# A state-space convolution with a 4-bit feed-forward on one core: reloads on another queue, a lag between chains, filler matmuls, earlier tables and staggered last chains

## The chip, the core and the metric

One core of one Trainium2 chip. The metric is device time of one execution in microseconds (us); lower is better. The engines are called by what they do in this kernel: TensorE (PE in the profile) runs matmuls, VectorE (DVE), ScalarE (ACT) and GpSimd (POOL) do elementwise work, SyncE (SP) issues transfers. ScalarE and GpSimd can issue transfers too.

## The reference, cut to what matters

```python
# x: [32, 64, 1024]; H = 64 heads, L = 1024, N = 64 states; lengths per batch row
K = 2 * real(einsum('hn,hnl->hl', Cs, exp(dtA * arange(L))))     # kernel of each head
y = causal_convolution(x * mask, K) + x * mask * D               # by FFT in the reference
y = y * mask
gate = y @ Wg;  up = y @ Wu                                      # 1024 x 2752, 4-bit, groups of 128
inter = gate * sigmoid(gate) * up
out = x + float16(inter @ Wd)                                    # 2752 x 1024, 4-bit, groups of 128
```

The rows of the products are the 2048 pairs (head, batch row), and their columns run along the 1024 positions.

## The kernel before, in words

Work is held with positions on partitions and the 2048 pairs along the free axis, cut into four blocks of 512 (16 heads each). A convolution is a product with Toeplitz tiles: the head's kernel is computed in factors (`tables` and `factors` on VectorE and ScalarE, `make_kernel` on TensorE), written to a padded DRAM tensor `kpad`, and read back as a Toeplitz tile `t0` of 512 KB per head (`toeplitz`, by SP). `conv_head` does 24 matmuls of a head; after every second head the pair is masked and split into a high and a low float16 part (`xh`, `xl`).

The weights are unpacked to 8 bits, and scales are applied in PSUM: a chain accumulates one group of 128 rows (four matmuls of 128x512), then VectorE or ScalarE multiplies the PSUM tile by the ratio of two scales, and the next group is added. `gu_one` and `gu_pair` are chains of gate and up, `dn_pair(k, blk, place)` is a chain of the down product: 256 of the 1024 output rows (k from 0 to 3) for block `blk`, 22 groups. Its inputs are `ihl` (21 groups, high and low parts, one block at a time) and `ic` (the last group). The chains of gate and up make the products of two blocks at once. Those of the first go into `ihl`, those of the second into the DRAM tensor `spill`. When the fourth chain of block 0 (or 2) has passed group g, `dn_pair` issues a reload of `ihl[:, g]` from `spill` (256 KB) for block 1 (or 3), and the chains of that block wait, in the order in which the program is written, until the reload of their group has been issued.

`roll` writes that order out: it takes chains from a list, holds three in PSUM (four in the stages called wide, when convolutions do not need the banks), and lets each do one group in turn. Between the groups it lets side work go on at given rates. Stage 0 and 1 are gate and up chains of one block; 2 the pairs for blocks 0 and 1; 3 and 4 the down chains of blocks 0 and 1, with the convolutions of blocks 2 and 3 (heads 32 to 63) at their side; 5 the pairs for blocks 2 and 3; 6 and 7 the down chains of blocks 2 and 3. A planner (`dve`, `act`, `pe`, with fixed costs) decides only which engine gets each rescale.

Ahead of `roll` lies the lead: the parameters, the kernels of heads 0 to 15, the convolution of block 0 with other work hung in at given steps (`events`), and matmuls without a use that keep TensorE occupied (`busy`). Heads 16 to 31 run at the side of stage 0; the tables and the kernel of heads 24 to 31 are `group_24`. At the end of a down chain the scaled result `o` is added to the residual `xr` and stored.

The lines of the profile: 524 is the Toeplitz load, 547 the matmul of a head, 617 and 619 the rescale of a pair chain, 636 and 639 that of the other chains, 679 and 680 the matmuls of `gu_pair`, 723 and 724 those of `dn_pair`, 731 the reload, 742 to 744 the output, 750 the residual load, 424 and 426 the matmuls of `make_kernel`, 866 the filler. Tile `chq` is a chain's PSUM tile, `cq` that of two heads, `kq` that of a kernel.

Of the kernel before, what the change touches and what calls it, by code (L numbers as in the profile page):

```python
# [10 lines left out]
F16 = mybir.dt.float16  # L11
F8 = mybir.dt.float8e4
# [5 lines left out]
ALU = mybir.AluOpType  # L18
# [6 lines left out]
GH, GI = 8, 22  # L25
# [6 lines left out]
MAGIC = 12582912.0  # L32
RATES = {"first": (0.5, 4.6), "fill": (1.0, 0.8), "convs": 1.9}
HOP, MM, LANDING = 220.0, 215.7, 6000.0
DVE_ROOM, ACT_ROOM = 1200.0, 1500.0
LOG2E = 1.4426950408889634
LN2_HI = 0.693359375
# [126 lines left out]
def decay_tables(nc, pool, co, cst, h0):  # L164
    xd = pool.tile([128, 8, 64], F32, name=f"xd{h0 // 8}", bufs=1, tag=f"xd{h0 // 8 % 4}")
    for h in range(8):
        nc.scalar.activation(xd[:, h, :], cst[:, 0:64], AF.Exp, scale=co["na"][:, h0 + h:h0 + h + 1])
    return xd
# [89 lines left out]
class Core:  # L258
# [451 lines left out]
    def dn_pair(self, k, blk, place):  # L710
        nc = self.nc
        q = self.psum("chq", place)
        ready = self.bank(place)
        for g in range(GI):
            while blk % 2 == 1 and g < 21 and not self.loaded.get((blk, g)):
                yield
            if g in (0, 8, 16):
                self.need(("dn", k, g // 8))
            self.pe((4 if g < 21 else 2) * MM, ready)
            for j in range(2):  # L720
                lw = self.wd[k][:, g, 128 * j:128 * j + 128]
                if g < 21:
                    nc.tensor.matmul(q[:, j], lw, self.ihl[:, g, 0], start=(g == 0), stop=False, skip_group_check=True)  # L723
                    nc.tensor.matmul(q[:, j], lw, self.ihl[:, g, 1], start=False, stop=False, skip_group_check=True)  # L724
                else:
                    nc.tensor.matmul(q[:, j], lw, self.ic[blk % 2], start=False, stop=True, skip_group_check=True)
            if g < 21:
                ready = self.rescale_two(q, self.rdn[:, 2 * k:2 * k + 2, g:g + 1])
                self.passed[blk, g] = self.passed.get((blk, g), 0) + 1
                if blk % 2 == 0 and self.passed[blk, g] == 4:  # L730
                    nc.gpsimd.dma_start(self.ihl[:, g], self.spill[g])
                    self.loaded[blk + 1, g] = True
                yield
        xr = self.res[k] if blk == 3 else self.residual(self.fw, 2 * k, blk)
        o = self.fw.tile([128, 2, 512], F16, name="o", bufs=2)
        self.bank_free[place].append(self.act(1180, self.tp + HOP) + HOP)
        for j in range(2):
            n = 2 * k + j
            if blk == 3 and j == 1 and k > 0:
                nc.vector.tensor_scalar(o[:, j], q[:, j], self.ldn[:, n:n + 1], None, ALU.mult)  # L740
            else:
                nc.scalar.activation(o[:, j], q[:, j], AF.Copy, scale=self.ldn[:, n:n + 1])
            (nc.gpsimd if blk < 3 or (j == 0 and k < 3) else nc.vector).tensor_tensor(xr[:, j], xr[:, j], o[:, j], ALU.add)
            (nc.gpsimd if blk < 3 else nc.sync).dma_start(self.io["out"][128 * n:128 * n + 128, 512 * blk:512 * blk + 512], xr[:, j])
        yield

    def residual(self, pool, n0, blk):
# [7 lines left out]
def roll(c, items, sides, wide):  # L755
    items, active = list(items), []
    used = {"a": 0, "b": 0}
    stage, credit = 0, {}

    def place(s):  # L760
        if used["b"] < PLACES["b", "pair"]:
            return "b"
        if s in wide and used["a"] == 0:
            return "a"
        return None

    def begin():
        nonlocal stage
        where = place(items[0][0]) if items else None
        if where is None:  # L770
            return None
        s, make = items.pop(0)
        if s != stage:
            c.forced = True
            for side, _, must in sides.get(stage, ()):
                for _ in side if must else ():
                    pass
            stage, c.forced = s, False
        if where == "a":
            c.banks("a", "pair")  # L780
        used[where] += 1
        active.append([s, make(where), where, 0])
        return active[-1]

    recent = []

    def round_of():
        if items:
            return list(active)
        resting = recent[-2:] if len(active) > 2 else recent[-1:]  # L790
        return [min((a for a in active if a not in resting or len(active) == 1), key=lambda a: a[3])]

    while items or active:
        begin()
        for a in round_of():
            recent.append(a)
            a[3] += 1
            try:
                next(a[1])
            except StopIteration:  # L800
                active.remove(a)
                used[a[2]] -= 1
                new = begin()
                if new:
                    new[3] += 1
                    next(new[1])
            now = min([o[0] for o in active] + [stage])
            if now not in wide and used["a"] == 0:
                c.banks("a", "single")
            for side, rate, paced in sides.get(now, ()):  # L810
                credit[side] = min(credit.get(side, 0.0) + rate, 2.0 if paced is None else 99.0)
                while credit[side] >= 1 and (paced is not None or c.room()):
                    credit[side] -= 1
                    next(side, None)
# [3 lines left out]
def tile_ssm_ffn(ctx, tc, io):  # L818
    nc = tc.nc
    c = Core(ctx, tc, io)  # L820
# [13 lines left out]
    kg_stack = ExitStack()  # L834
    kg = kg_stack.enter_context(tc.tile_pool(name="kg", bufs=1))
# [22 lines left out]
    xd = [decay_tables(nc, kg, co, c.cst, h0) for h0 in (0, 8)]  # L858
# [4 lines left out]
    def busy(h0, n):  # L863
        e1, e2 = (e.rearrange("p h n -> p (h n)") for e in c.fac[h0])
        for _ in range(n):
            nc.tensor.matmul(c.psum("wq", "b")[:, 0, :128], e1, e2, start=True, stop=True)
# [11 lines left out]
    c.masks()  # L878
    tc.no_sync_barrier()

    def ratios_gu():
        c.rgu, c.lgu = c.scale_ratios(c.sgu, NT, GH, "gu", [
            (0, 21, 0, 128, 1.0), (21, 42, 0, 128, 0.0625), (42, 43, 0, 64, 1.0), (42, 43, 64, 128, 0.0625)])
# [17 lines left out]
    def load_16():  # L901
        c.us[4] = c.conv_load(16)

    events = {7: kernel_8, 56: ratios_gu, 87: load_16, 75: lambda: c.make_kernel(kg, 16, 8, "b")}
    for i, _ in enumerate(c.conv(0)):
        if i in events:
            with c.after("dve" if i == 56 else None):
                events[i]()
        if i % 8 == 0 and 32 <= i <= 104:
            next(unpack_it)  # L910

    def second():
        with c.after("dve"):
            ratios_dn()
        for h in range(16, 22):
            c.t0[h] = c.toeplitz(h)
        for h in range(16, 32):
            forced, c.forced = c.forced, True
            while h >= 22 and 24 not in c.known:
                next(group_it)  # L920
            c.forced = forced
            yield from c.conv_head(h)

    def group_24():
        yield from c.tables(kg, 24, 8)
        yield from c.factors(kg, 24, 8, xd[3])
        for _ in range(2):
            yield
        c.make_kernel(kg, 24, 8, "a")
        yield  # L930
        kg_stack.close()
        wdp = ctx.enter_context(tc.tile_pool(name="wdp", bufs=1))
        c.wd = [wdp.tile([128, GI, 256], F8, name=f"wd{k}") for k in range(4)]
        yield

    group_it = group_24()

    def third():
        tiles = [c.cv.tile([128, 2, L], F16, name="t0", bufs=3) for _ in range(3)]
# [66 lines left out]
    def residuals():  # L1006
        take = c.scratch(c.x[0])
        c.res = [c.residual(take, n0, 3) for n0 in (0, 2, 4, 6)]
        yield

    convs_it = convs()
# [10 lines left out]
    def one(s, b):  # L1022
        return [(s, lambda where, i=i: c.gu_one(i, b, where)) for i in range(4)]

    def pairs(s, i0):
        order = [ct for i in range(i0, 21) for ct in (i, 21 + i)] + [42]
        chains = [(s, lambda where, ct=ct: c.gu_pair(ct, where)) for ct in order]
        if s == 2:
            for at, h0 in ((34, 40), (30, 32)):
                chains.insert(at, (s, kernel_item(h0)))  # L1030
        return chains
# [4 lines left out]
    items = one(0, 0) + one(1, 1) + pairs(2, 4) + down(3, 0) + down(4, 1) + pairs(5, 0) + down(6, 2) + down(7, 3)  # L1036
# [63 lines left out]
```

## Time and profile before

| | |
|---|---|
| Time of the runs | 1098.02 us median of 3 (1097.51 to 1101.98) |
| Profiled execution | 1101.47 us, its span 1099.7 us, mean granted clock 0.985 |
| TensorE busy | 1030.9 us, 94% |
| VectorE, ScalarE, GpSimd busy | 817.5, 760.1, 275.9 us |
| Chain that ended last | PE 72%, DVE 10%, DMA 6%, ACT 6%, issue 5% |
| Reloads | 42 of 256 KB on GpSimd's queue, median 3.0 us from issue to landing |
| Toeplitz loads to `t` | 48 of 512 KB on SP's queue, median 4.1 us |

A window row gives, for a stretch of the span, the busy time of each engine and how many instructions it ran, then the clock granted to TensorE (1.00 is full), the share of time in which the transfer engines were busy, and GB/s. A timeline row gives start, duration, engine, line, operation, tiles, and in brackets how long the engine had been idle before and what ended that. The rows of waits give who waited for whom, the total, how many times, and the longest. The end of a matmul is modelled; back to back, matmuls of 128x512 start every 0.216 us, though each is shown as 0.38.

### The profile page before, as it was taken

The page shows a single profiled execution, that of the slowest core. Times are in us where ns is not written, and L with a number is a line of the kernel's source. Part 1 is how long each engine was busy: PE and PEld are TensorE (multiplying, and loading weights), DVE is VectorE, ACT ScalarE, POOL GpSimd, SP SyncE. Part 2 cuts the span into 40 slices and gives each one's busy share as a digit, 9 for nine tenths or more (in the row PEclk, how much of TensorE's full clock was granted, in tenths as well). Part 3 has the DMA queues.
Part 4 walks back from the last instruction along what each step waited for, and adds up shares of the span by engine and source line. Part 5 has one row for each costly group of instructions (what it writes and reads, how often), then busy time and mean ns, then how long its engine had stood idle before and what let it go on. Part 6 is the DMA issues. An engine that isn't in the chain of part 4 may idle for free.

```text
span 1099.7 us, 15366 instructions
## 1 busy us (share of the span) xinstructions
PE 1030.9 (94%) x5834; PEld 515.0 (47%) x5834; DVE 817.5 (74%) x925; ACT 760.1 (69%) x1008; POOL 275.9 (25%) x323
## 2 busy tenths in 40 slices
PE   3898999999999999998898999999999999999995
PEld 3766434444444445653555444444444444444442
DVE  8875779878998876676454777777777777877775
ACT  5755777878777778675475767666666666778774
POOL 0323233333324341132123113222222222114201
PEclk9899999999999999998999999999999999999998
DMA  6966311111212233355554001000000000424202
GB/s 204 321 227 198 107 68 58 58 61 46 77 58 69 67 103 120 116 184 162 175 182 153 20 29 68 20 20 20 20 20 20 20 20 23 150 77 135 77 1 77
DMA packets 49410, 99.74 MB, mean 91 GB/s; under 512 B 9524, under 2 KB 11444, under 8 KB 49336
## 3 DMA queue, kind: packets, MB, share of 16 engines
q1 hardware_dynamic: 39576, 70.38, 19.9%
q0 software_dynamic: 8640, 28.32, 7.4%
q8 instruction: 45, 0.74, 0.3%
q14 instruction: 29, 0.24, 0.1%
q10 hardware_dynamic: 1120, 0.07, 0.1%
HBM read 78.99 MB, written 19.76 MB: 90 GB/s over the span
## 4 chain that ended last, share of the span: by engine, by line
PE 72%; DVE 10%; DMA 6%; ACT 6%; issue 5%; POOL 1%; DVEq 0%; ACTq 0%; POOLq 0%; SPq 0%
PE chq L679 20%; PE chq L680 20%; PE chq L723 12%; PE chq L724 12%; PE cq L547 4%; DVE chq L617 2%; DMA ihl<-spill 2%; DMA t<-kpad 2%; PE chq L656 2%; PE chq L657 2%; ACT chq L639 1%; DVE v L692 1%; ACT sg L687 1%; ACT chq L619 1%; DMA ihl<-kpad 1%
## 5 line engine op out<-in xcount | busy, mean ns | idle before, releaser
L679 PE MATMUL chq<-xh,w 128*128 128x512 f16 x1216 | 459.8, 379 | 9.3 <-DVE chq L617 4.1
L680 PE MATMUL chq<-xl,w 128*128 128x512 f16 x1216 | 458.6, 379 | 0.0
L617 DVE TENSOR_SCALAR chq<-chq,gur 128x1024 f32<-128x1024 f32 x260 | 332.1, 1289 | 89.1 <-PE chq L680 88.4
L619 ACT ACTIVATE chq<-chq,gur 128x1024 f32<-128x1024 f32 x286 | 305.0, 1085 | 84.1 <-PE chq L680 83.8
L639 ACT ACTIVATE chq<-chq,dnr 128x512 f32<-128x512 f32 x344 | 225.0, 661 | 85.5 <-PE chq L724 79.8
L723 PE MATMUL chq<-ihl,wd 128*128 128x512 f16 x672 | 257.9, 384 | 16.4 <-DMA ihl<-spill 12.0
L636 DVE TENSOR_TENSOR chq<-chq,dnr 128x1024 f32<-128x1024 f32 x164 | 201.3, 1231 | 96.3 <-PE chq L724 92.3
L724 PE MATMUL chq<-ihl,wd 128*128 128x512 f16 x672 | 257.1, 384 | 0.0
L680 PEld LDWEIGHTS <-w 128*128 128x128 fp8e4 x1216 | 118.7, 98 | 159.8 <-issue 23.4
L679 PEld LDWEIGHTS <-w 128*128 128x128 fp8e4 x1216 | 118.8, 98 | 143.4
L309 POOL TENSOR_TENSOR ihl<-v,ihl 128x512 f16<-128x512 f32 x42 | 48.3, 1149 | 333.2 <-ACT ihl L628 333.2
L723 PEld LDWEIGHTS <-wd 128*128 128x128 fp8e4 x672 | 66.3, 99 | 84.0 <-DMA ihl<-spill 13.5
L547 PEld LDWEIGHTS <-t 128*128 128x128 f16 x1152 | 82.8, 99 | 43.4 <-DMA t<-kpad 10.4
L724 PEld LDWEIGHTS <-wd 128*128 128x128 fp8e4 x672 | 66.3, 99 | 74.5 <-issue 10.7
L547 PE MATMUL cq<-uh,t 128*128 128x64 f16 (+6 forms) x720 | 90.6, 226 | 7.6 <-DMA t<-kpad 7.4
L547 PE MATMUL cq<-ul,t 128*128 128x256 f16 (+3 forms) x360 | 71.9, 226 | 0.0
L628 ACT CAST ihl<-v 128x512 f16<-128x512 f32 x42 | 25.9, 617 | 61.5 <-DVE v L692 58.1
L564 POOL TENSOR_TENSOR xl<-y,xh 128x512 f16<-128x512 f32 x28 | 33.7, 1204 | 112.6 <-ACT xh L562 112.6
L692 DVE SCALAR_TENSOR_TENSOR v<-chq,gul,sg 128x1024 f32<-128x1024 f32 x38 | 48.6, 1279 | 17.7 <-ACT sg L687 9.9
L309 POOL TENSOR_TENSOR spill<-v,spill 128x512 f16<-128x512 f32 x42 | 48.7, 1159 | 15.7 <-ACT spill L628 15.6
L687 ACT ACTIVATE sg<-chq,gul 128x1024 f32<-128x1024 f32 x38 | 42.3, 1113 | 14.4 <-PE chq L680 12.9
L639 ACT ACTIVATE chq<-chq,gur 128x512 f32<-128x512 f32 x58 | 37.7, 660 | 19.1 <-PE chq L657 15.5
(247 smaller groups left out, 820.8 us busy)
## 6 DMA issues: line engine op xcount, KB each, us to landing
t<-kpad SPq DMA_DIRECT2D x48, 512.0 KB, 4.1
spill<-spill POOLq DMA_DIRECT2D x42, 256.0 KB, 2.3
ihl<-spill POOLq DMA_DIRECT2D x42, 256.0 KB, 3.0
z<-zc SPq DMA_DIRECT2D x29, 256.0 KB, 3.7
u<-xF SPq DMA_DIRECT2D x12, 512.0 KB, 3.7
xr<-xT SPq DMA_DIRECT2D x12, 512.0 KB, 5.0
out<-xr POOLq DMA_DIRECT2D x24, 256.0 KB, 2.5
w<-qgu SPq DMA_DIRECT2D x21, 256.0 KB, 4.2
```

What stands on the lines that cost most here:

```text
L309: self.nc.gpsimd.tensor_tensor(out, a, b, op)
L547: nc.tensor.matmul(q[:, d:, h % 2, :], t0[:, lw, 128 * d:128 * d + 128], uu[:, 0:8 - d, h % 4, :], start=(d == 0 and k == 0 and h % 2 == 0 ...
L617: self.mark("dve", self.nc.vector.tensor_scalar(q, q, col, None, ALU.mult))
L619: self.mark("act", self.nc.scalar.activation(q, q, AF.Copy, scale=col))
L636: self.mark("dve", self.nc.vector.tensor_tensor(q, q, cols.to_broadcast([128, 2, 512]), ALU.mult))
L639: self.mark("act", self.nc.scalar.activation(q[:, k], q[:, k], AF.Copy, scale=cols[:, k]))
L679: nc.tensor.matmul(q[:, b], lw, xh[:, g, :], start=(g == 0), stop=False, skip_group_check=True)
L680: nc.tensor.matmul(q[:, b], lw, xl[:, g, :], start=False, stop=(g == GH - 1), skip_group_check=True)
L687: nc.scalar.activation(sg, q, AF.Silu, scale=last)
L692: nc.vector.scalar_tensor_tensor(v, q, last, self.sg.pop(ct - 21), ALU.mult, ALU.mult)
L723: nc.tensor.matmul(q[:, j], lw, self.ihl[:, g, 0], start=(g == 0), stop=False, skip_group_check=True)
L724: nc.tensor.matmul(q[:, j], lw, self.ihl[:, g, 1], start=False, stop=False, skip_group_check=True)
```

## The change

Five edits. The reloads go out on ScalarE's queue in place of GpSimd's. A chain of block 1 or 3 waits until the reload two groups ahead of its own has been issued (`LAG`). Ten filler matmuls follow head 7 in the lead. `group_24` moves ahead of the loop over `c.conv(0)`: the tables of heads 24 to 31 are written out at six steps among heads 10 to 13 of the lead, and their kernel is made in stage 0 as soon as its factors are done. At the end, when no chain is left to start, `roll` no longer keeps the chains level but lets each of the last four stay two groups ahead of the one begun after it (`HEAD_START`); `o` of block 3 has tiles of its own in the freed `c.x[1]`; five of the eight last adds go to GpSimd (three before), and ScalarE stores the last output tile.

```diff
+LAG, HEAD_START = 2, 2
...
-            while blk % 2 == 1 and g < 21 and not self.loaded.get((blk, g)):
+            while blk % 2 == 1 and g < 21 and not self.loaded.get((blk, min(20, g + LAG))):
                 yield
...
                 if blk % 2 == 0 and self.passed[blk, g] == 4:
-                    nc.gpsimd.dma_start(self.ihl[:, g], self.spill[g])
+                    nc.scalar.dma_start(self.ihl[:, g], self.spill[g])
                     self.loaded[blk + 1, g] = True
...
-        o = self.fw.tile([128, 2, 512], F16, name="o", bufs=2)
+        o = self.fw.tile([128, 2, 512], F16, name="o", bufs=2) if blk < 3 else self.last_o([128, 2, 512], F16)
...
-            (nc.gpsimd if blk < 3 or (j == 0 and k < 3) else nc.vector).tensor_tensor(xr[:, j], xr[:, j], o[:, j], ALU.add)
-            (nc.gpsimd if blk < 3 else nc.sync).dma_start(self.io["out"][128 * n:128 * n + 128, 512 * blk:512 * blk + 512], xr[:, j])
+            (nc.gpsimd if blk < 3 or 2 * k + j < 5 else nc.vector).tensor_tensor(xr[:, j], xr[:, j], o[:, j], ALU.add)
+            (nc.gpsimd if blk < 3 else nc.scalar if 2 * k + j == 7 else nc.sync).dma_start(self.io["out"][128 * n:128 * n + 128, 512 * blk:512 * blk + 512], xr[:, j])
...
-        active.append([s, make(where), where, 0])
+        active.append([s, make(where), where, 0, HEAD_START * len(items)])
...
-        return [min((a for a in active if a not in resting or len(active) == 1), key=lambda a: a[3])]
+        return [min((a for a in active if a not in resting or len(active) == 1), key=lambda a: a[3] - a[4])]
...
+    def group_24():
+        yield from c.tables(kg, 24, 8)
+        yield from c.factors(kg, 24, 8, xd[3])
-        for _ in range(2):
+        while c.forced:
+            yield
+        c.make_kernel(kg, 24, 8, "a")
...
-    events = {7: kernel_8, 56: ratios_gu, 87: load_16, 75: lambda: c.make_kernel(kg, 16, 8, "b")}
+    events = {7: kernel_8, 63: lambda: busy(4, 10), 56: ratios_gu, 87: load_16, 75: lambda: c.make_kernel(kg, 16, 8, "b")}
     for i, _ in enumerate(c.conv(0)):
...
+        if i in (80, 86, 92, 98, 104, 110):
+            next(group_it)
...
         c.res = [c.residual(take, n0, 3) for n0 in (0, 2, 4, 6)]
+        c.last_o = c.scratch(c.x[1])
```

More of the change, by code (lines that the diff above doesn't have):

```diff
@@ L879, in tile_ssm_ffn @@
     tc.no_sync_barrier()
+    def group_24():
[4 more added lines that the diff above has]
+        c.make_kernel(kg, 24, 8, "a")
+        yield
+        kg_stack.close()
+        wdp = ctx.enter_context(tc.tile_pool(name="wdp", bufs=1))
+        c.wd = [wdp.tile([128, GI, 256], F8, name=f"wd{k}") for k in range(4)]
+        yield
+    group_it = group_24()
     def ratios_gu():
@@ L922, in second @@
             yield from c.conv_head(h)
-    def group_24():
-        yield from c.tables(kg, 24, 8)
-        yield from c.factors(kg, 24, 8, xd[3])
-        for _ in range(2):
[L928 to L936, printed above, removed]
     def third():
```

## The prediction

> **What bounds the kernel now.** I read the busy shares first: TensorE (PE) is busy nearly all the time, so time can only come from its idle gaps, from stretches at a lower clock, and from the end.
>
> ```profile
> PE 1030.9 (94%) x5834; PEld 515.0 (47%) x5834; DVE 817.5 (74%) x925; ACT 760.1 (69%) x1008; POOL 275.9 (25%) x323
> ```
>
> Then PE's own waits (line and tile, what ended the wait, total us, times, longest), to see which transfers starve it:
>
> ```profile
> PE kq L426 <- DVE e1t L222: 15.1, 3, 13.3
> PE chq L723 <- DMA ihl<-spill: 12.0, 7, 3.5
> PE cq L547 <- DMA t<-kpad: 9.4, 6, 2.9
> ```
>
> The seven waits for reloads (12.0 us) all lie at 488 to 581 us, the six for Toeplitz loads at 40 to 111 and at 599. Stretches of 20 us there (PE, PEld, DVE, ACT, POOL busy, then PEclk, DMA share, GB/s), with one of the later stage 6 for comparison:
>
> ```profile
> 500.00:520.00 20.00, 17.16 (x84) 7.15 (x82) 11.48 (x18) 10.63 (x20) 5.36 (x8) 0.74 0.43 132
> 520.00:540.00 20.00, 14.14 (x120) 8.46 (x119) 9.27 (x13) 7.81 (x13) 2.80 (x4) 0.91 0.61 192
> 580.00:600.00 20.00, 16.77 (x162) 11.49 (x161) 6.50 (x7) 11.51 (x18) 9.67 (x11) 1.00 0.52 174
> 600.00:620.00 20.00, 20.00 (x99) 9.28 (x97) 13.38 (x12) 12.66 (x17) 3.43 (x4) 0.91 0.08 28
> 980.00:1000.00 20.00, 20.00 (x94) 9.11 (x93) 14.79 (x12) 15.57 (x24) 4.43 (x8) 1.00 0.28 79
> ```
>
> The clock column matters as much as the idle: 0.74 and 0.91 mean that part of the stretch ran at half clock. In the timeline PE shows how that starts:
>
> ```profile
> 506.87 0.39 PE L723 MATMUL chq<-ihl,wd 128*128 128x512 f16 x1 [2.84 <-DMA ihl<-spill]
> ...
> 509.57 0.63 PE L724 MATMUL chq<-ihl,wd 128*128 128x512 f16 x1
> ```
>
> After a gap of 2.84 us the same matmul goes from 0.38 to 0.63 us. In finer stretches PEclk is 0.50 at 43.6-50.3 (after a gap of 2.10), 507.9-518.2 (2.84), 524.5-528.2 (3.48) and 600.2-603.4 (2.87); gaps up to 1.74 started none. The Trainium skill ("TensorE: Matmul & The Clock Gate", HAM oscillation) says to avoid gaps above about 3.4 us; the trace disagrees, since 2.10 us sufficed, and the measurement decides.
>
> **The change part by part.** The sum is made against the profiled execution (1101.47 us, span 1099.7), which lies 3.45 above the median 1098.02 of the runs (1097.51 to 1101.98).
>
> *Reloads through ScalarE, lag of two.* Today GpSimd issues them, in order behind adds and stores of other chains: the reload of the third group went out at 495.32, the fourth only at 502.94, because a subtraction, two adds (1.16 each) that waited 2.32 for ScalarE and a store stood before it. Landing takes 2.8/3.0/6.6 us (min/median/max). The chain of block 1 reads a group one round, 12 to 16 matmuls of 0.216 (2.6 to 3.5 us), after the last chain of block 0 has read it, so a landing just misses. In the changed order that distance is 28 matmuls or more through the starved part, and some 46 (heads included), 6 to 7 us, after it. That covers the worst landing plus an issue of 0.41 (ScalarE's four kpad stores) to 0.57 (its two larger ones). So I take off all 12.0 us. With the 2.84 and 3.48 gaps go the half-clock stretches behind them: 10.3 us, half of it lost, 5.1; and PE's work from 525.36 to 528.2 at half, 1.4. That is 6.5.
>
> The gap of 2.87 at 599 is another chain: store of a finished chain (GpSimd 586.42 and 588.46), then SP's residual load at 592.66, which waits for it, then the Toeplitz load queued behind on SP (593.13), landing 598.9. In the changed order PE has 12 more matmuls before it needs that tile, 12 x 0.216 = 2.6 us; and the 3.2 us at half clock behind the gap cost 1.6. Together 4.2.
>
> What is late next: PE arrives sooner at the kernel of heads 56 and at the heads from 48. From the end of head 47, VectorE runs nine table steps (5.2 us) before its next rescale, so a chain waits about 1.8; factors of 56 are ready at about +11.0 where PE comes at +10.7; the Toeplitz tile of head 48 (factor copy at +6.4, store, load 2.2 later as at 515.27 to 517.43, landing 4 to 5) arrives at about +13 where PE comes at +11.9. Sum 3.2, less the 0.73 of a similar wait at 520.9: 2.5 back. Stage 4: 12.0 + 6.5 + 4.2 - 2.5 = 20.2 gained. If these next steps take what they took before (y at 508.4 to the factor at 524.9: 16 us), PE waits 5.3 instead of 0.3 and falls into half clock (1.6 to 5.1): the gain is then 10 to 13.
>
> Who stands behind a reload on ScalarE: the rescales of the chains. It waits for the last chain's matmul, which ends before those that the next rescales need, so its own wait delays none. In stage 6 a round is 16 matmuls, 3.45 us, with two rescales of 1.36 on ScalarE: 0.73 is free per reload, and 0.41 to 0.57 fits. It costs nothing; at the longest issue of SP's queue (1.09 for a Toeplitz load) it would cost 21 x 0.36 = 7.6. Stage 6 has nothing to win: PE is at 20.00 of 20. GpSimd's 42 x 0.55 us are freed off the path. The Trainium skill ("DMA: Bandwidth & Descriptors", Issuing engines are not separate DMA queues) says another issuer saves only the time to initiate a transfer; this trace cannot show a reload on ScalarE, and by that rule the lag earns the gain, with the same sum.
>
> *Filler in the lead.* Ten matmuls of 128x128 f32: sixteen records of them took 3.72 us (17.99 to 21.71), 0.2325 each, so twenty take 4.65. They start at 40.23, cover the wait of 2.10 for the Toeplitz tile of head 8, and push head 8 back by 2.55. The clock stays up, which returns 3.3 (half of 6.7). But the end of the lead is not PE's: the tile of head 16 arrives at 60.6 by kernel 16 (PE 46.14 to 48.12), its store (49.68 to 56.16, with DMA at a share of 1.05 until 54) and its load. Kernel 16 would end at 48.4, 0.3 later. PE is done at 58.3 instead of 59.04 and waits 2.6 instead of 1.56: above the 2.10 that dropped the clock, where 1.56 did not. Bounds for that: 0, and 3.3 as after 2.10; I take the shortest half-clock stretch seen, 1.6. Together +1.9 (0.3 to 3.6). By the Trainium skill's figure of 3.4 us (the same page and section) neither the old wait nor the new one is long enough to change the clock, and the lead would come to +0.3.
>
> *Tables of heads 24 to 31 among the heads.* In the old place PE waits 0.98 for factors (84.42) and 0.90 and 1.52 for two Toeplitz loads (91.78, 94.98). In the changed order the kernel matmuls stand some 80 matmuls earlier, about 7 us, and the loads follow. The table steps (about 4.4 us) go to 50-60, where VectorE is idle 5.5. Just before the kernel matmuls VectorE has 4.4 us of work while PE has 4.6, so up to 0.5 of a new wait: -2.9 (-3.4 to 0).
>
> *Tail.* Before, four chains end together: last matmul 1087.1, last add 1093.5. Staggered, the last steps run with two chains and one. A chain's step needs 0.65 to its last matmul, 0.38 for it, about 0.06, and a rescale of 1.23 (VectorE) or 1.36 (ScalarE): 2.35 to 2.45. Three chains fill 2.59 of PE; two 1.73, one 0.86. Laying out the last 54 matmuls so gives some 5.0 of PE idle against 0.61, PE end +4.4. After it, one chain is left: ScalarE 0.69, add 0.69, VectorE's scaling 0.75, add 0.69, in series on VectorE, about 2.7 against 6.4 before. Net +0.5 (-1 to +2). More adds on GpSimd, the separate output tile and ScalarE's last store lie inside that.
>
> Sum: 1101.47 - 20.2 + 1.9 - 2.9 + 0.5 = 1080.8. Carrying over the whole 3.45 by which the profiled execution is above the median gives 1077.3; half-clock stretches are part of what differs between executions, and part of them is already taken off, so I take the middle, **1079**.
>
> **The rivals.** *Next waits take half.* The pipeline to kernel 56 and head 48 is the bound once reloads are not; worked above, a loss of 7 to 10 more: about 1088. For it: VectorE's table steps are in line with rescales; against: much of the old 16 us was ScalarE waiting for a PE at half clock.
> *ScalarE is held.* If a reload holds ScalarE for h, issue and waiting for its semaphores, stage 6 pays 21 x (h - 0.73). Stage 4 has a round of 4.1 us with ScalarE about two thirds busy, and pays 21 x (h - 1.3). It is over 0.5% slower than before from h = 1.6 (18.3 + 6.3 = 24.6, so 1103.6); at 1.8, 1079 + 22.5 + 10.5 = 1112. For it: reloads and SP's loads are chained by shared completion semaphores, and a Toeplitz landing lasts up to 10.2 us. Against: those stand some ten microseconds ahead in the order, and no issue row is above 1.09.
> *The lag does nothing.* If chains that wait only reorder, and loads are late for DMA bandwidth, it stays within 0.5% of 1098 (about what a measurement can tell from no change). Against: DMA share is 0.43 to 0.61 there.
>
> **How the numbers follow.** Forecast 0.66, half gain 0.16, held 0.12, no difference 0.06. Above 0.5% faster (below 1092.5) are the first two: 0.82; same 0.06; slower 0.12. The forecast's own range is 1069 to 1086 (clock after the filler 0 to 3.6, tables 0, tail 2, the 3.45); the half-gain case carries it to 1092, which leaves 0.2 out.
>
> **What would show it.** Right: no wait for the reload, PEclk 1.00 in 500-540; wait at head 16 grown to about 2.6; no waits at kernel 24; PE idle near 5 in the last 15 us, and a shorter rest after it. Wrong: ScalarE's rescales starting late behind a reload in stage 6, or a gap above 2 before head 48.

## The result, and the profile after

| | before | after |
|---|---|---|
| Median of the runs | 1097.76 us (1093.58 to 1101.98, 4) | 1084.60 us (1081.11 to 1085.59, 4) |
| Ratio, 95% interval | | 0.9874 (0.983 to 0.9919) |
| Profiled execution | 1101.47 (span 1099.7) | 1081.11 (span 1079.3) |

The forecast was 1079.0 in a range of 1069 to 1092. The two profiled executions differ by 20.4 us, the medians by 13.2: before's profiled execution is near the slowest of its runs, after's is the fastest of its own. The lines named so far stand one later in the changed kernel (723 is now 724, and so on).

Busy shares of the changed kernel; TensorE has lost 7.6 us of busy time although the filler added some, since a matmul at half clock counts as busy for longer:

```profile
PE 1023.3 (95%) x5854; PEld 511.1 (47%) x5854; DVE 807.2 (75%) x913; ACT 771.8 (72%) x1025; POOL 255.7 (24%) x283
```

What TensorE waited for (line and tile, what ended the wait, total us, times, longest):

```profile
PE kq L427 <- DVE e1t L223: 14.8, 3, 13.2
PE chq L724 <- DVE chq L637: 4.8, 6, 2.2
PE chq L680 <- DVE chq L618: 4.2, 6, 1.0
PE kq L425 <- DMA ihl<-dpad: 3.7, 1, 3.7
PE cq L548 <- DVE y L560: 3.6, 1, 3.6
PE cq L548 <- DMA t<-kpad: 3.4, 3, 1.9
```

The 12.0 us of waits for reloads are gone altogether, and of the 9.4 for Toeplitz loads 3.4 are left. Two rows are new. One is 3.6 us for `y` of block 0, in the lead. The other is the row of rescales (L637): its longest wait, 2.2, lies at 487 us, where VectorE's table steps stand ahead of a rescale.

The same stretches of stage 4 as before, with one of stage 6 (busy time of PE, PEld, DVE, ACT, POOL, then PEclk, DMA share, GB/s):

```profile
500.00:520.00 20.00, 18.32 (x158) 10.40 (x156) 14.92 (x26) 15.01 (x27) 0.66 (x2) 1.00 0.68 209
520.00:540.00 20.00, 20.00 (x159) 11.98 (x158) 10.37 (x10) 14.07 (x22) 2.30 (x2) 1.00 0.62 208
580.00:600.00 20.00, 19.90 (x129) 10.45 (x128) 14.19 (x13) 12.90 (x18) 4.58 (x5) 1.00 0.16 61
600.00:620.00 20.00, 20.00 (x94) 9.02 (x93) 15.09 (x13) 15.25 (x20) 2.81 (x3) 1.00 0.08 27
980.00:1000.00 20.00, 19.91 (x93) 8.89 (x92) 13.95 (x12) 15.96 (x26) 10.29 (x12) 1.00 0.60 187
```

The clock column reads 1.00 where it read 0.74 and 0.91, and in 520 to 540 TensorE runs 159 matmuls where it ran 120. Stage 6 stays full with ScalarE issuing the reloads (980 to 1000). The issue itself, by the source line of the reload (count, then ns min/median/max), and its landing:

```profile
L732 ACTq DMA_DIRECT2D ihl<-spill x42: 326/326/348, 481.9 to 997.5; - x42
...
DMA to landing us min/median/max: 2.4/2.8/6.2
```

At the end, the chain of waits now closes with one chain instead of four (us, duration, engine, tile, line):

```profile
1072.18 1.02 PE chq L727 x2
...
1073.23 0.70 ACT xh L743
...
1075.34 0.69 DVE xl L744
```

From TensorE's last matmul to the end of the span it is 6.1 us (1073.2 to 1079.3) against 12.6 before (1087.1 to 1099.7). TensorE in exchange idled 4.4 us in the steps ahead of it, 2.9 of them in two waits of 1.45.

To compare executions I use the 42 spill stores that GpSimd issues, two blocks of 21, as marks. They cut a run into a lead (to the second store), a first steady part (2nd to 21st, 261.2 to 261.5 us in every run, the kernel before included), the stage with the first 21 reloads (21st to 22nd), a second steady part (22nd to 42nd, 303.3 to 303.9 in every run) and a tail (42nd to the end of the span). All differences lie in three columns:

| kernel | 2nd store at | 21st to 22nd | tail | span |
|---|---|---|---|---|
| before | 149.5 | 229.7 | 155.9 | 1099.7 |
| after, three executions | 146.6, 147.5, 147.6 | 211.2, 211.2, 210.0 | 156.7, 157.1, 156.6 | 1079.3, 1080.8, 1079.0 |
| neither | 147.3 | 221.9 | 155.1 | 1088.9 |
| queue_only | 147.3 | 220.7 | 155.4 | 1088.1 |
| lag_only | 148.2 | 212.2 | 156.4 | 1081.4 |
| nofill | 148.7 | 212.2 | 157.0 | 1082.6 |
| oldtab | 149.3 | 210.6 | 157.0 | 1082.1 |
| level | 147.9 | 211.7 | 156.9 | 1081.3 |
| hold2 | 148.6 | 217.6 | 161.3 | 1092.1 |
| hold4 | 146.7 | 225.1 | 181.6 | 1118.0 |
| later | 144.6 | 211.6 | 157.2 | 1078.0 |
| best | 146.1 | 210.9 | 159.6 | 1081.3 |

The marks are not quite the same in all kernels. With the lag TensorE runs five matmuls fewer between the 21st and the 22nd store (1491 for 1496) and six more behind the 42nd (662 for 656). At 0.216 each, about 1.1 us leave the second column and 1.3 us enter the tail without any change in the work. Each row but "after" is one execution.

### The profile page after: what moved, and what is told of

It reads as the page before. It is cut to its first block, busy times and chain, and to the rows that moved or that the text cites. A ratio compares the mean times of both kernels' runs of the same rounds, so it can differ in the third digit from the quotient of the medians.

```text
span 1079.3 us, 15408 instructions
## 1 busy us (share of the span) xinstructions
PE 1023.3 (95%) x5854; PEld 511.1 (47%) x5854; DVE 807.2 (75%) x913; ACT 771.8 (72%) x1025; POOL 255.7 (24%) x283
## 3 DMA queue, kind: packets, MB, share of 16 engines
q1 hardware_dynamic: 39432, 70.12, 20.2%
## 4 chain that ended last, share of the span: by engine, by line
PE 76%; DVE 11%; ACT 6%; DMA 3%; issue 3%; POOL 0%; SPq 0%; DVEq 0%; ACTq 0%
PE chq L680 20%; PE chq L681 20%; PE chq L724 12%; PE chq L725 12%; PE cq L548 6%; DVE chq L618 2%; PE chq L657 2%; PE chq L658 2%; ACT chq L640 2%; DVE v L693 1%; ACT sg L688 1%; DMA t<-kpad 1%; ACT chq L620 1%; DVE chq L637 1%; DMA ihl<-xF 1%
## 5 line engine op out<-in xcount | busy, mean ns | idle before, releaser
L618 DVE TENSOR_SCALAR chq<-chq,gur 128x1024 f32<-128x1024 f32 x257 | 328.4, 1290 | 88.6 <-PE chq L681 87.8
L640 ACT ACTIVATE chq<-chq,dnr 128x512 f32<-128x512 f32 x350 | 228.1, 661 | 74.5 <-PE chq L725 68.4
L637 DVE TENSOR_TENSOR chq<-chq,dnr 128x1024 f32<-128x1024 f32 x161 | 197.3, 1231 | 99.1 <-PE chq L725 95.0
L640 ACT ACTIVATE chq<-chq,gur 128x512 f32<-128x512 f32 x66 | 43.2, 661 | 12.3 <-PE chq L658 11.1
L310 POOL TENSOR_TENSOR spill<-v,spill 128x512 f16<-128x512 f32 x42 | 48.6, 1158 | 14.1 <-ACT spill L629 13.9
L688 ACT ACTIVATE sg<-chq,gul 128x1024 f32<-128x1024 f32 x38 | 42.2, 1112 | 11.5 <-PE chq L681 11.1
```

The source lines that it names most:

```text
L310: self.nc.gpsimd.tensor_tensor(out, a, b, op)
L618: self.mark("dve", self.nc.vector.tensor_scalar(q, q, col, None, ALU.mult))
L637: self.mark("dve", self.nc.vector.tensor_tensor(q, q, cols.to_broadcast([128, 2, 512]), ALU.mult))
L640: self.mark("act", self.nc.scalar.activation(q[:, k], q[:, k], AF.Copy, scale=cols[:, k]))
L688: nc.scalar.activation(sg, q, AF.Silu, scale=last)
```

## The experiments

My theory after the first result was that lag and queue each earn a part of the stage with the reloads, that the lead's edits are worth about nothing, and that the stagger costs up to 1.5 us. The rivals were the lag alone, the queue alone, and a ScalarE that reloads hold up.

### Lag and queue apart: again, queue_only, lag_only, neither

The four ran on one chip and share the runs of the kernel before (1095.72 us). The changed kernel itself:

> The changed kernel once more, as the reference for the three beside it. First comparison: 1084.6 us against 1097.8, 13.2 less; its profiled execution took 1081.1 with 2.1 us lost to half clock. Theory: 1081 to 1086, no wait of TensorE for a reload, and a gap of 3.5 to 4 us near 54 us (block 0's head waits for VectorE) in this execution too.

It took 1082.84 us, ratio 0.9895 (0.9865 to 0.9924). The gap near 57 us was there with 3.75 us.

`queue_only` drops the lag:

```diff
-LAG, HEAD_START = 2, 2
+LAG, HEAD_START = 0, 2
```

> Reloads stay on ScalarE, but a chain of block 1 may be ordered as soon as its own group's reload is (lag 0). Theory (lag and queue each do a part): the reload that went out 7.6 us late on GpSimd now goes out in time, but a landing of 2.4 to 2.8 us plus 0.33 of issue still just misses a round of 2.6 to 3.5, so several waits of 0.3 to 2 us stay, 3 to 6 us in sum, with one or two stretches at half clock: 4 to 9 us slower than the changed kernel. Rival 'the lag alone earns it' (another issuer saves only the time to initiate): waits of about 12 us as before, 13 to 18 us slower. Rival 'the queue alone earns it': within 3 us of the changed kernel.

`lag_only` keeps the lag and gives the reloads back to GpSimd:

```diff
-                    nc.scalar.dma_start(self.ihl[:, g], self.spill[g])
+                    nc.gpsimd.dma_start(self.ihl[:, g], self.spill[g])
```

> Lag of two groups, but GpSimd issues the reloads again. Theory (each a part): the lag gives 6 to 7 us of distance; a reload that sits 5 to 7.6 us behind adds and stores of GpSimd and then lands in 2.8 to 3.0 is late once or twice: 2 to 4 us of waits for reloads, 3 to 7 us slower than the changed kernel. Rival 'the lag alone earns it': no wait above 0.5 us for a reload, within 3 us of the changed kernel. Rival 'the queue alone earns it': 10 us or more slower.

`neither` has both edits:

> Reloads on GpSimd and no lag, all else as in the changed kernel: the stage from 411 to 640 us is then as before. Theory: seven or so waits for reloads of about 12 us with half clock behind the long ones, span from the store at 411 to that at 640 about 18 us longer than in the changed kernel; 14 to 20 us slower than it in the median, which is 1 to 5 us above the kernel before (lead and tail of the change then give nothing). Rival 'the lead's part gave most': 8 us or less slower than the changed kernel.

Measured medians, with ratios to the kernel before:

| | reloads on GpSimd | reloads on ScalarE |
|---|---|---|
| lag 0 | neither: 1090.41, 0.9955 (0.9934 to 0.9975) | queue_only: 1090.07, 0.9958 (0.9934 to 0.9983) |
| lag 2 | lag_only: 1080.76, 0.9870 (0.9838 to 0.9902) | after: 1082.84, 0.9895 (0.9865 to 0.9924) |

The lag takes off 9.6 us on GpSimd's queue and 7.2 on ScalarE's. The queue takes off 0.3 without the lag and adds 2.1 with it, both inside the intervals. `queue_only` alone would have borne out my theory of two parts (7.2 slower than the changed kernel, with 3.1 us of waits for reloads). The other two refute it: `lag_only` is 2.1 us faster where 3 to 7 slower was expected, and `neither` is 7.6 slower where 14 to 20 was expected, hardly more than `queue_only`. The lag earns the gain alone. The waits for reloads, one line each from `neither`, `queue_only` and `lag_only`:

```profile
PE chq L724 <- DMA ihl<-spill: 8.8, 6, 2.1
```

```profile
PE chq L724 <- DMA ihl<-spill: 3.1, 3, 1.7
```

```profile
PE chq L724 <- DMA ihl<-spill: 2.8, 1, 2.8
```

ScalarE does remove most of the waits for reloads by itself (8.8 to 3.1), yet the time stays. The stage is 220.7 us instead of 221.9: other gaps take their place, such as 2.62 for a rescale at 489, 0.97 at 513, and 1.37 and 2.09 for Toeplitz loads at 519 and 588. The lag leaves one wait of 2.8 on GpSimd's queue, and the stage still takes 212.2. So it is the order of the chains that counts, more than the transfer.

One of these new gaps comes with the queue. At 481 to 486 us VectorE's table steps stand ahead of a rescale, while GpSimd works off adds and stores. In `after`, and then in `lag_only` (VectorE's step, then GpSimd at that time):

```profile
483.19 2.96 DVE L204 SCALAR_TENSOR_TENSOR xl<-xl,cst 128x256 f32<-128x256 f32 x1
483.58 1.17 POOL L565 TENSOR_TENSOR xl<-y,xh 128x512 f16<-128x512 f32 x1
484.70 1.16 POOL L744 TENSOR_TENSOR xr<-xr,o 128x512 f32<-128x512 f32 x1
```

```profile
484.56 0.47 DVE L204 SCALAR_TENSOR_TENSOR xl<-xl,cst 128x256 f32<-128x256 f32 x1
484.37 0.56 POOL L745 DMA_DIRECT2D out<-xr  x1 [0.30 <-POOL xr L744]
484.92 0.55 POOL L732 DMA_DIRECT2D ihl<-spill  x1
```

With the reload off its queue, GpSimd runs two elementwise operations back to back while VectorE is in this step, and the step takes 2.96 us; with the reload on it, GpSimd issues transfers during the step, and it takes 0.47. It is 2.95 to 2.96 in all ten executions with reloads on ScalarE and 0.47 in all four with reloads on GpSimd. TensorE's wait for the rescale behind it is 2.20 in the changed kernel and 0.63 in `lag_only`. That this is why ScalarE's queue brings nothing is likely from these rows, but no run tests it; the move also changes the written order of TensorE's matmuls at some places of this stage.

How little that order needs: written out, the lag makes the first chain of block 1 yield one turn at its very start, and from there on the chains keep their distance by themselves. A lag of one gives the same program, instruction for instruction, as a lag of two, and so does a lag in block 1 alone.

Against the kernel before, `neither` still gains 5.3 us (1095.72 to 1090.41), which should be the worth of the lead, the tables and the tail together. In the two profiles the lead and the tail are only 2.2 and 0.8 us shorter; where the other 2.3 of the medians lie is not shown.

### The parts of the lead and the tail: nofill, oldtab, level

These ran on another chip (before: 1099.93 us). `nofill`:

```diff
-    events = {7: kernel_8, 63: lambda: busy(4, 10), 56: ratios_gu, ...
+    events = {7: kernel_8, 56: ratios_gu, ...
```

> The changed kernel without the twenty filler matmuls. Theory (filler is worth nothing, since the lead's end is set by loads and by VectorE, not by TensorE): the gap of 2.1 us before head 8 comes back with half clock behind it, the gap near 54 to 58 us (3.2 to 3.7 us, for VectorE's y) shrinks by about as much, the first spill store stays at 141 to 144 us, and the time is within 2 us of the changed kernel. Rival 'it costs what was predicted' (1.9): first store near 140.5, 2 us faster. Rival 'the filler saves the clock': first store at 145 to 147, 3 us slower.

`oldtab`:

```diff
-        while c.forced:
+        for _ in range(2):
             yield
...
-        if i in (80, 86, 92, 98, 104, 110):
-            next(group_it)
```

> Tables and factors of heads 24 to 31 back in their old place, all else as in the changed kernel. Theory (the early tables took away 3.4 us of waits at 84 to 95 us and the 1.74 behind them at 150 us, and put VectorE's table steps ahead of block 0's y): the waits 0.98, 0.90, 1.52 and 1.74 come back, the wait for y near 57 us goes from 3.2 to 3.7 down to below 1, and the second spill store is 0 to 3 us later than the 147 to 148 of the changed kernel; the time is within 3 us. Rival 'the wait for y is the filler's or older': it stays above 3 us, and the time is 4 to 5 us longer.

`level` has `LAG, HEAD_START = 2, 0`:

> The last four chains advance together as before (head start 0), all else as in the changed kernel. Prediction for the stagger: +0.5 us, PE idle 4.4 to 5 us and a rest shorter by 3.7. Theory: the tail (last spill store to the end of the span, 155 to 157 us in the changed kernel, 155.9 in the kernel before) becomes 154.5 to 156, the four waits of 0.4 and the two of 1.45 go, the rest behind the last matmul grows from about 5 to 11 us; 0 to 1.5 us faster than the changed kernel. Rival 'the stagger pays': tail 158 or more, 2 us or more slower.

Measured: nofill 1086.11, ratio 0.9890 (0.9857 to 0.9922); oldtab 1086.63, 0.9890 (0.9859 to 0.9921); level 1082.94, 0.9858 (0.9822 to 0.9893). None can be told from the changed kernel, whose three ratios are 0.9868 to 0.9895. The traces say more. In `nofill` (start, duration, line, tiles, and in brackets the idle time before):

```profile
44.21 1.25 PE L548 MATMUL cq<-ihl,t 128*128 128x256 f16 x12 [0.79 <-DMA t<-kpad]
...
55.02 1.68 PE L548 MATMUL cq<-ihl 128*128 128x256 f16 x24 [0.87 <-DVE y L560]
...
60.77 0.28 PE L548 MATMUL cq<-uh,t 128*128 128x256 f16 x1 [2.54 <-DMA t<-kpad]
...
64.72 0.58 PE L657 MATMUL chq<-xh,w 128*128 128x512 f16 x1 [2.65 <-ACT xh L563]
```

The gap of 2.10 before head 8, which the filler was to cover, was expected back with half clock behind it; it is 0.79 here, with none. The gap for `y` shrinks to 0.87, from 3.6 to 3.8 in the changed kernel and 2.5 to 4.2 in the nine runs with its whole lead. But gaps of 2.54 and 2.65 stand behind it, and the second store comes at 148.7: 1.2 later than the 147.5 that those nine runs average (146.6 to 148.6). The filler is worth nothing that these runs can tell apart; it did not cost the 1.9 predicted.

In `oldtab` two of the three old gaps at 84 to 95 us are back:

```profile
55.16 1.68 PE L548 MATMUL cq<-ihl 128*128 128x256 f16 x24 [1.20 <-DVE y L560]
...
60.34 0.28 PE L548 MATMUL cq<-uh,t 128*128 128x256 f16 x1 [1.97 <-DMA t<-kpad]
...
85.71 0.69 PE L427 MATMUL kq<-e2t,e1t 128*32 128x32 f32 x16 [0.98 <-DVE e1t L223]
...
93.79 0.28 PE L548 MATMUL cq<-uh,t 128*128 128x256 f16 x1 [1.62 <-DMA t<-kpad]
```

The wait for `y` is 1.20, less than in any of the nine, so the early tables (and, by `nofill`, the filler) reshape that gap. The second store comes at 149.3, 1.8 later than that average. The wait of 1.74 at 150 us of the kernel before does not come back here, nor in any other of these runs; what removed it stays open.

`level` ends with a tail of 156.9, not the 154.5 to 156 expected, and in the middle of the 156.6 to 157.1 of the staggered kernel: the idle time saved on TensorE is paid back behind it. The stagger is worth nothing.

### What a reload costs ScalarE: hold4, hold2

```diff
-                    nc.scalar.dma_start(self.ihl[:, g], self.spill[g])
+                    for p in range(0, 128, 32):
+                        nc.scalar.dma_start(self.ihl[p:p + 32, g], self.spill[g, p:p + 32])
```

> Each reload goes out as four transfers of 32 partitions, all on ScalarE: four issues in place of one, about 4 x 0.33 = 1.3 us of ScalarE per reload if an issue holds it that long. By the prediction's price (0.73 free per reload in the last stage) this pays 21 x 0.57 = 12 us between the last spill store and the end, so 12 us slower than the changed kernel, and ScalarE's rescales start late behind the reloads. Rival: an issue runs beside ScalarE's activations (in the trace the reloads at 481.90 and 508.76 do) and holds nothing: within 2 us of the changed kernel.

It took 1119.85 us, 1.0194 (1.0163 to 1.0225): slower than the kernel before. Its tail grew by 24.7 us, twice what was expected, and the stage with the reloads by 13.9. ScalarE in the last stage:

```profile
1000.20 0.78 ACTq L733 DMA_DIRECT2D ihl<-spill  x2
1000.66 0.66 ACT L640 ACTIVATE chq<-chq,dnr 128x512 f32<-128x512 f32 x1
1001.03 0.90 ACTq L733 DMA_DIRECT2D ihl<-spill  x2
1003.14 0.66 ACT L640 ACTIVATE chq<-chq,dnr 128x512 f32<-128x512 f32 x1 [1.83 <-DMA ihl<-spill]
```

The issues split the rescales (L640), and one rescale starts 1.83 us late behind a reload; there are four such waits in the run, 8.5 us in all, on top of the issue time. With two transfers of 64 partitions each:

> Each reload goes out as two transfers of 64 partitions on ScalarE. With four transfers a reload cost 24.7 us over 21 reloads behind the last store, 1.17 each beyond the 0.73 that are free, so 0.48 for each transfer. Theory (the price is the number of transfers times 0.48, and a round has 0.73 free): 0.95 per reload, 0.22 over, 21 x 0.22 = 4.7 us more tail (161 to 162 instead of 157), and nothing in the stage from 411 to 640 us, where 1.3 is free: 4 to 5 us slower than the changed kernel. Rival (ScalarE is blocked only when transfers queue up four deep): tail within 1 us of the changed kernel's.

It took 1093.92 us against 1082.40 of the changed kernel on the same chip; ratio to before 0.9978 (0.9955 to 1.0). The tail is 161.3: 4.4 more, with 4.7 expected. The stage with the reloads is 217.6: 6.4 to 7.6 more, where nothing was expected. The issue by source line:

```profile
L733 ACTq DMA_DIRECT2D ihl<-spill x84: 451/452/1052, 483.7 to 1010.2; - x84
```

Two issues of 0.452 make 0.90, that is 0.17 above the free 0.73, or 3.6 us in 21 reloads. So the price rule of the prediction comes close in the last stage as long as ScalarE waits for no landing, and one issue of 0.33 fits with 0.4 to spare. In stage 4 the rule does not hold: the stage is longer although two issues are less than the 1.3 that I had called free. TensorE's waits for Toeplitz loads are 4.7 us there, against 1.1 to 2.4 in the changed kernel, and those for rescales some 1.6 more; how the second issue leads to them was not followed. The Trainium skill ("DMA: Bandwidth & Descriptors", Rules for kernel authors) says not to bother with two transfers to disjoint partition halves, since they serialize. The runs agree that it does not pay: a half lands no sooner than a whole reload (2.8 us in the median for both), and the split costs 11.5 us here.

### Mending the gap in the lead, and a combination: again2, later, best

In the trace of after, VectorE stands in order before an unpack that waits for its weights, with `y` behind it:

```profile
52.44 0.49 DVE L584 TENSOR_SCALAR w<-w,cst 128x1024 uint16<-128x1024 uint16 x1 [2.46 <-DMA w<-qgu]
...
54.31 1.74 DVE L510 TENSOR_TENSOR ul<-u,uh 128x1024 f16<-128x1024 f32 x1
55.98 0.68 DVE L560 TENSOR_TENSOR y<-cq,mask 128x512 f32<-128x512 f32 x1
```

The reference for this chip (before: 1097.43 us):

> The changed kernel a third time, as the reference beside the three others on this chip: 1081 to 1087 us, no wait of TensorE for a reload, gap of 2.5 to 3.7 us for VectorE's y near 57 us, tail (last spill store to the end of the span) 156.5 to 157.2.

It took 1082.40, ratio 0.9868 (0.9843 to 0.9894). `later` moves the unpacking:

```diff
-        if i % 8 == 0 and 32 <= i <= 104:
+        if i % 8 == 0 and 40 <= i <= 112:
             next(unpack_it)
```

> The unpacking of the weights begins one step later (at 40 instead of 32), so that VectorE does not stand before an unpack that waits about 2.5 us for its load while block 0's y is behind it. All else as in the changed kernel. Theory (that wait on VectorE is what starves TensorE at 54 to 57 us): the gap for y falls from 2.5 to 3.7 below 1.5, its half clock goes, and the first spill store comes 1 to 3 us earlier than 142 to 143.5. Rival (the lead is a chain of loads and VectorE work, as without filler and with the old tables, where gaps only changed places): gaps of the same sum appear at 60 to 66 us for the Toeplitz tile of head 16 and for xh, and the first store stays within 1 us.

```profile
54.71 1.68 PE L548 MATMUL cq<-ihl 128*128 128x256 f16 x24 [1.81 <-DVE y L560]
...
59.49 0.27 PE L548 MATMUL cq<-uh,t 128*128 128x256 f16 x1 [1.58 <-ACT r L207]
...
62.82 0.38 PE L657 MATMUL chq<-xh,w 128*128 128x512 f16 x1 [1.84 <-ACT xh L563]
```

The gap falls from 3.76 to 1.81 (below 1.5 was expected), with no half clock behind it, and the second store comes at 144.6, 3.0 earlier than in the run beside it. Of these 3.0, 1.1 stand already at 29 us, ahead of the moved step (the first execution of the changed kernel is 0.9 ahead there too), so the step is worth about 1.9. The theory held in part: 1.58 of new wait appeared at 59, and the unpack still waits 1.64 for its weights. The median, 1080.95, ratio 0.9860 (0.9834 to 0.9887), is 1.5 us lower than the changed kernel's; the intervals overlap. `best` combines `later` with reloads on GpSimd and level chains:

> The combination that the runs so far point to: lag of two with GpSimd issuing the reloads (ratio 0.9870 to the kernel before, against 0.9895 with ScalarE), last chains level (0.9858), and unpacking one step later. Theory (none of these three matters by more than 2 us): 1079 to 1084, within 3 us of the changed kernel; one wait of up to 2.8 for a reload may come back. Rival (each gives its difference in full, 2 to 4 us each): 1074 to 1078.

1082.45 us, 0.9876 (0.9846 to 0.9906): nothing is added up. Its lead is 1.5 us early, but its tail is 159.6, of which 9.1 us lie between the last addition and the end of the span (5.7 in `level`); why was not followed up. No version here is shown to beat the changed kernel.

## Why the prediction was right, and where it was not

**Reloads and lag, -20.2: right mechanism, mis-sized.** The waits for reloads and the half clock behind them went, as said. Between the two profiles the stage is 18.5 us shorter (229.7 to 211.2), which seems to bear out the size too. But `neither`, whose instructions stand in this stage in the same order on every engine as in the kernel before, takes 221.9 there, with 8.8 us of waits for reloads instead of 12.0 and 3.4 us lost to half clock instead of about 8. So up to 8 us of the terms -12.0, -6.5 and -4.2 were a mishap of the one execution that had been profiled (5 to 6 if the 2.3 us of the medians that the lead and the tail leave open belong to this stage). Undoing this part costs 10.7 us of the stage in the profile, 1.1 of it a shift of the marks, and 7.6 in the median. The size is near that of the rival "next waits take half", but not for its reason: the factors of head 56 made no wait in the three executions of the changed kernel. The sum should have been made from what the median execution loses, and the 3.45 us by which the profile lay above the median was the hint.

**Which half earns it.** The prediction gave both halves the credit for "all 12.0" and said that by the rule of the Trainium skill ("DMA: Bandwidth & Descriptors", Issuing engines are not separate DMA queues) the lag would earn it, with the same sum. `lag_only` and `queue_only` agree with that rule: issue 0.55 on GpSimd, 0.33 on ScalarE, landing 3.0 and 2.8, and no gain from the queue that the intervals show.

**New waits, +2.5.** The rescale behind VectorE's table steps was put at about 1.8 and measured 2.20 and 0.76; the Toeplitz tile of head 48 at 1.1, measured 1.1, 2.4 and 1.4 in three executions. Both are where the prediction put them, and 1 to 2 us longer in sum than the 3.2 said. So a sign that the prediction had named for being wrong, a gap above 2 before head 48, did show. One likely reason is a term that it put at nothing: GpSimd's time for the issues, "freed off the path". With it freed, GpSimd's elementwise work fell on VectorE's table steps, of which two took 2.13 and 2.96 us at 481 to 486; with the reloads on GpSimd the second took 0.47.

**Stage 6 on ScalarE, 0.** Right, and for its reason: the stretch stays full, since an issue takes less than the 0.73 that is free. It takes 0.33; the 0.41 to 0.57 of the prediction were halves of rows that merge two issues and the time between them, and SP's longest Toeplitz issues were 1.14 and 1.39, not 1.09. The price beyond 0.73 came to 4.4 in `hold2`, where 4.7 had been worked out from `hold4`. `hold4` itself cost 24.7 where the prediction's price gave 12. So the rival "ScalarE is held" is a real mechanism: `hold4` is slower than the kernel before, with ScalarE held for landings as well as for issues.

**Filler, +1.9: not borne out.** Without it the second store comes 1.2 later, not earlier. The failing step is the wait at head 16, "2.6 instead of 1.56": it measured 1.93 in the first execution and under 0.6 in the next two, and TensorE had lost 3.6 to 3.8 us before it, waiting for `y`. That wait was not foreseen. The tables were to go "to 50-60, where VectorE is idle 5.5"; part of that idle time was VectorE standing before a load, with `y` next in its order. Work put there does not fill the idle time but lengthens the line.

**Tables, -2.9.** The waits at 84 to 95 us went as said, and in `oldtab` they came back at 0.98 and 1.62. By the second store the early tables are worth 1.8.

**Tail, +0.5.** The prediction's own terms, +4.4 and 2.7 against 6.4, make +0.7. TensorE idled 4.4 (said: 5.0), and from its last matmul to the last addition it is 2.8 (said: 2.7). The output store behind that became shorter too, 3.3 instead of 6.2, which I had not counted. Yet the tail grew by 0.7 to 1.2. By `level` the stagger itself neither costs nor gains: TensorE ends 5.8 us later behind the last spill store, and 6.0 less follow. The tail is 155.1 and 155.4 in the two kernels with the stagger and without the lag; the six matmuls that the lag brings behind the 42nd store, 1.3 us, make up most of that difference.

**Sum.** Predicted from the median: 19 less; measured 13.2, 12.9 and 15.0 on three chips. In the one comparison that splits it, 7.6 came with lag and queue (predicted 20.2) and 5.3 with the rest (predicted 0.5), of which the profiles show 3.0. The total came out within 6 us since the first was too large and the second too small: the mechanism was right, the closeness of the sum was luck.

## What to carry to other kernels

Where a consumer just misses its transfers, let it start one turn later: that costs nothing if other work can fill the turn, and it helped more than a faster queue. Before summing the waits of one profile, see how that execution stands to the median: stretches at half clock come and go between executions of one program. Idle time on an engine is free for new work only if what ends the wait is not followed, in the engine's order, by something that the bottleneck needs. And work taken off an engine moves what follows it: look at what the freed engine will do next, and beside whom.

## What the runs showed of the hardware that was not expected

The same gap starts half clock in one execution and not in another. Three executions of the same program have the same gap of 3.63 to 3.76 us near 57 us, and of 2.20 at 487 to 488. The stretches behind them (columns as above: PE's busy time first, PEclk third from the end), in the first execution:

```profile
57.50:61.50 4.00, 2.42 (x42) 2.27 (x39) 3.84 (x6) 2.21 (x4) 3.07 (x3) 1.00 0.96 303
488.50:491.50 3.00, 3.00 (x8) 1.04 (x8) 1.05 (x1) 1.11 (x3) 0.25 (x1) 0.50 0.99 376
```

and in the second (`again`):

```profile
57.50:61.50 4.00, 3.67 (x32) 3.23 (x32) 4.00 (x7) 2.08 (x3) 2.23 (x2) 0.58 0.79 233
488.50:491.50 3.00, 2.25 (x19) 1.14 (x19) 2.36 (x3) 0.86 (x2) 1.05 (x2) 1.00 0.86 273
```

The third is as the second. The longer gap left the clock alone in one of three, and the shorter one (with one of 0.76 right behind it) dropped it in one of three. In `hold4` a gap of 1.55 was followed by half clock from 29.2 us on, and in the tails gaps of 1.45 with shorter ones ahead of them, at 1071 us in the changed kernel. So my rule (2.10 does, 1.74 does not) was read from one execution and is wrong as a threshold. Ahead of the tails, half clock comes in these traces in pieces of 3.41 us, or of two or three times that (6.83, 10.24). The Trainium skill ("TensorE: Matmul & The Clock Gate", What's actually happening) describes a window of about 3.4 us that runs freely, whatever the kernel does; a chance of phase agrees with that. Its rule of no gap above about 3.4 us (HAM oscillation) is no safe bound here, by the 2.20 and the 1.55.
